# Seven products of a 2 x 2 block matmul, joined in two PSUM accumulators instead of four, and used for eight more columns of fc

## The chip, the core and the metric

The kernel runs on one core of a Trainium2 chip. Five engines work from queues of their own, each in the order in which the program issued its work: TensorE (PE, matmul), VectorE (DVE), ScalarE (ACT), GpSimd (POOL) and SyncE (SP, which here only issues DMAs). They wait for each other through semaphores. The metric is the device time of one execution in microseconds; lower is better. Before the change it is 803.75 us (median of three runs, 800.14 to 804.41).

## The reference

A cross-attention block on 4 batches, 512 query rows, 512 context rows, width 512, 16 heads of 32, inner width 2048, all in float32:

```python
x = layer_norm(hidden_states, ln1_w, ln1_b)
q, k, v = x @ q_w + q_b, enc @ k_w + k_b, enc @ v_w + v_b      # 16 heads of 32
attn = softmax(where(mask, q @ k.T / sqrt(32), min))
hidden = (attn @ v) @ cproj_w + cproj_b + hidden_states
y = layer_norm(hidden, ln2_w, ln2_b)
y = gelu(y @ fc_w + fc_b, approximate=True)                    # fc: 512 -> 2048
return hidden + y @ proj_w + proj_b                            # proj: 2048 -> 512
```

## The kernel before

**Attention.** The work is cut into 16 groups `w` (batch `w // 4`, four heads each) and each group into four query tiles `qt` of 128 rows: 64 *units* `u = 4 w + qt`. Each unit does, in this order of issue:

- `attend` (L331), in some units only: 16 matmuls that multiply exchanged probabilities of an earlier half group with v, and a VectorE multiply into `oT`;
- `scores` (L255): four matmuls into `sc`, four banks of PSUM of which there is one set (L259), so that the next unit's scores wait until VectorE has read all four. VectorE adds the mask and takes the row's extreme (L266), ScalarE takes the exponential (L270), four times each;
- `turn` (L274): VectorE transposes the probabilities; in odd units ScalarE makes `rr` (L292), and the *exchange* (L303, L314) sends 16 DMAs on SP that move blocks between partitions;
- *filler*: other TensorE work that hides the softmax. The lists `first[w]` and `later[w]` (L798 to L881) say by hand which work goes into which unit. A tuple gives one list for each `qt`; a plain list is spread over the group by the costs `CHAIN` and `TURN` (L718) and due times (L904 to L909).

Filler is made of the k, q and v products of later groups (`prep_k`, `prep_q`, `prep_v`), transposes, the output projection of a finished batch (`cproj`), and the MLP of batch 0 and half of batch 1 (`mlp`, L812 to L815). `some(n)` (L817) takes the next n matmul chains of the MLP; a pair of fc columns counts as two. `SPLIT` is 1: batch 0's whole MLP and the first half of batch 1's lie inside attention; the rest follows in `last_mlps` (L590).

**The MLP's fc.** The layer-normed rows, turned, are in `yT`; f counts 16 blocks of 128 columns of fc. There are two ways to compute it:

- `fc` (L532), for the first eight blocks of batch 1: one chain of four 128x512 matmuls a block, then gelu on ScalarE straight from PSUM (L537).
- `fc_seven` (L483), for *pairs* c of blocks: the 256 columns and 512 rows are seen as a 2 x 2 block product, for which seven products of half-size blocks do instead of eight. Each product is two 128x256 matmuls (L495). The weights' sums s1 to s4 are made by GpSimd in attention (`fc_sums`, L520, two pairs ahead) and by VectorE after it (`sum_wa`, L580); the sums t1, t2, t3, t4 of `yT` by `y_sums` (L472). t3 takes the place of a block of `yT`.

In `fc_seven` the seven products go into four PSUM tiles: q1; q2 and q6; q5 and q7; q3 and q4. ScalarE copies q1 to SBUF (L498), VectorE joins the rest in four sums (L501 to L509), and ScalarE applies gelu to two 128x512 halves (L513). In attention the tiles come from `ps_acc` (four banks, shared with every other chain), after it two come from `ps_acc` and two from `ps_last` (four banks). A PSUM tile of 512 floats is one bank.

`fc_by_pair` (L543) calls it in attention, `fc_pair` (L608) after it. `proj` (L551) is the second half of the MLP in attention (accp, L554); after attention `project` (L613) does it with seven products too.

**Queues that matter for the change.** GpSimd's queue also holds `v_bias` (L252), row sums on loaded rows (`add_row`, L357, which waits for the DMA of `load_hid`, L397), the layer norm's scale (`ln_rs`, L131) and some DMA issues. SP's queue holds all weight loads (`load_mlp`, L437, L444), `load_hid` (L402) and the exchanges (L328). ScalarE's table for the exponential and that for gelu alternate, with a table load each time.

**Batch 1 in attention.** In units 52 to 63 the filler is: five chains of proj of batch 0 (units 52 to 55), one more (56), then one fc chain in unit 57, two in 58, one in each of 59 to 62, one and a proj chain in 63. After the last unit come the other seven proj chains of batch 1, among them the last two attends.

Of the kernel before, what the change touches and what calls it, by code (L numbers as in the profile page):

```python
# [12 lines left out]
F32 = mybir.dt.float32  # L13
U8 = mybir.dt.uint8
AF = mybir.ActivationFunctionType
# [5 lines left out]
P = 128  # L21
# [4 lines left out]
ND = D // P  # L26
# [4 lines left out]
FQ = NF // NQ  # L31
# [3 lines left out]
SPLIT = 1  # L35
FIRST = 2
# [11 lines left out]
LN1W, LN1B, QB, KB, LN2W, LN2B, FCB = 0, 4, 8, 12, 16, 20, 24  # L48
# [4 lines left out]
def xattn_block(ctx: ExitStack, tc: tile.TileContext, x, encT, mask, q_w, k_w, v_w, c_w, fc_w, p_w, vecs, rows, out):  # L53
    nc = tc.nc
    scale = float(np.float32(1.0) / np.sqrt(HD).astype(np.float32))

    def pools(stack, **bufs):
        return [stack.enter_context(tc.tile_pool(name=n, bufs=k)) for n, k in bufs.items()]

    const, keep, hids, tiles, small = pools(ctx, const=1, keep=1, hids=6, tiles=4, small=4)  # L60
# [9 lines left out]
    vec = const.tile([P, NVEC], F32, tag="vec", name="vec")  # L70
# [3 lines left out]
    qb = const.tile([P, NG], F32, tag="qb", name="qb")  # L74
# [6 lines left out]
    gT = [gt[:, i * FQ * L : (i + 1) * FQ * L].rearrange("p (k l) -> p k l", k=FQ) for i in range(2)]  # L81
# [8 lines left out]
    ys = const.tile([P, 3, 2, L // 2], F32, tag="ys", name="ys")  # L90
# [6 lines left out]
    def mlp_w(n):  # L97
        n = n % MW + MW
        return pbt[:, n * D : (n + 1) * D]
# [16 lines left out]
    S = {}  # L116
    count = [0, 0, 0, 0, 0]
    Q = [nc.sync]

    def acc_tile(name):  # L120
        return ps_acc.tile([P, D], F32, tag="acc", name=name)
# [275 lines left out]
    def load_hid(b, ts_):  # L397

        for t in ts_:
            if ("hid", b, t) not in S:  # L400
                S["hid", b, t] = hids.tile([P, D], F32, tag="hid", name=f"hid_{b}_{t}")
            Q[0].dma_start(out=S["hid", b, t], in_=S["xa", b][ts(t, P), :])  # L402
        for t in ts_:
            add_row(S["hid", b, t], 1)

    def stat2(b, t):
        ln_stat((2, b), t, S["h", b, t])

    def norm2(b, t):
        h = S["h", b, t]  # L410
        y = tiles.tile([P, D], F32, tag="xn", name=f"xn2_{b}_{t}") if stays(b, t) else h
        S.setdefault(("yn", b), {})[t] = y
        ln_norm((2, b), t, y, h)
# [23 lines left out]
    def load_mlp():  # L437

        while count[0] < len(weights) and (count[0] < MW or weights[count[0] - MW][3] < count[1]):
            name, b, f, _ = weights[count[0]]  # L440
            w = mlp_w(count[0])
            if name == "fc":
                w = w.rearrange("p (d f) -> p d f", d=ND)
            Q[0].dma_start(out=w, in_=fc_w[:, f, :, :] if name == "fc" else p_w[ts(f, P), :])  # L444
            S[name + "w", b, f] = w
            count[0] += 1

    NP = NF // 2
    HL = L // 2

    def sub(o, x0, x1, engine=None):
        (engine or nc.vector).tensor_tensor(o, x0, x1, ALU.subtract)  # L452

    def add(engine, o, x0, x1):
        engine.tensor_tensor(o, x0, x1, ALU.add)  # L455
# [13 lines left out]
    def y_blocks(b):  # L469
        return [S["yT", b][:, 2 * k : 2 * k + 2, j * HL : (j + 1) * HL] for k in range(2) for j in range(2)]  # L470

    def y_sums(b):  # L472
        y11, y12, y21, y22 = y_blocks(b)
        e = nc.vector if b else nc.gpsimd
        sub(ys[:, 0], y12, y11)
        sub(ys[:, 1], y22, ys[:, 0])
        sub(y12, y22, y12, e)
        sub(ys[:, 2], y21, ys[:, 1], e)

    def acc_half(name):  # L480
        return acc_tile(name).rearrange("p (i l) -> p i l", i=2)

    def fc_seven(b, c, g, a, s, half):  # L483

        y11, t3, y21, y22 = y_blocks(b)
        t1, t2, t4 = (ys[:, i] for i in range(3))
        s1, s2, s3, s4 = s
        q1, q26 = (acc_half(f"{n}_{b}_{c}") for n in ("q1", "q26"))
        q57, q34 = (half(f"{n}_{b}_{c}") for n in ("q57", "q34"))
        p1 = small.tile([P, HL], F32, tag="p1", bufs=1, name=f"p1_{b}_{c}")  # L490
        g = g.rearrange("p i (j l) -> p (i j) l", j=2)

        def product(o, x, y):
            for k in range(2):
                nc.tensor.matmul(o, x[:, k], y[:, k], start=(k == 0), stop=(k == 1))  # L495

        product(q1[:, 0], a[0][:, 0:2], y11)
        nc.scalar.copy(p1, q1[:, 0])  # L498
        product(q26[:, 0], a[0][:, 2:4], y21)
        product(q26[:, 1], s2, t2)  # L500
        add(nc.vector, g[:, 0:4:3], q26, p1[:, None, :].broadcast_to([P, 2, HL]))  # L501
        product(q57[:, 1], s3, t3)
        product(q57[:, 0], s1, t1)
        u2 = g[:, 3:4]
        add(nc.vector, g[:, 1:3], q57, u2.broadcast_to([P, 2, HL]))
        add(nc.vector, g[:, 3], q57[:, 0], g[:, 2])
        product(q34[:, 0], s4, y22)
        product(q34[:, 1], a[1][:, 2:4], t4)
        add(nc.vector, g[:, 1:3], q34, g[:, 1:3])  # L509
        for i in range(2):  # L510
            f = 2 * c + i
            h = g[:, 2 * i : 2 * i + 2]
            nc.scalar.activation(h, h, AF.Gelu_apprx_tanh, bias=vec[:, FCB + f : FCB + f + 1], scale=1.0)  # L513

    fc_pairs = [(b, c) for b in range(SPLIT) for c in range(NP)]

    def raw_pair(b, c):
        return [S["fcw", b, 2 * c + i] for i in range(2)]

    def fc_sums():  # L520

        while count[3] < len(fc_pairs) and count[3] < count[4] + 2:
            b, c = fc_pairs[count[3]]
            if ("fcw", b, 2 * c + 1) not in S:
                return
            x, y = raw_pair(b, c)
            s = wsum[:, count[3] % 2]
            a_sums(x[:, :2], x[:, 2:], y[:, :2], y[:, 2:], s[:, 0], s[:, 1], y[:, :2], s[:, 2], nc.gpsimd)
            S["ws", b, c] = s[:, 0], s[:, 1], y[:, :2], s[:, 2]
            count[3] += 1  # L530

    def fc(b, f):  # L532
        q, k = divmod(f, FQ)
        acc = acc_tile(f"accf_{b}_{f}")
        for d in range(ND):
            nc.tensor.matmul(acc, S["fcw", b, f][:, d, :], S["yT", b][:, d, :], start=(d == 0), stop=(d == ND - 1))  # L536
        nc.scalar.activation(  # L537
            gT[q % 2][:, k, :], acc, AF.Gelu_apprx_tanh, bias=vec[:, FCB + f : FCB + f + 1], scale=1.0
        )
        count[1] += 1  # L540
        load_mlp()

    def fc_by_pair(b, c):  # L543
        q, k = divmod(2 * c, FQ)
        fc_seven(b, c, gT[q % 2][:, k : k + 2, :], raw_pair(b, c), S["ws", b, c], acc_half)
        count[1] += 2
        count[4] += 1
        load_mlp()
        fc_sums()
# [40 lines left out]
    def last_mlps():  # L590
# [76 lines left out]
                add(nc.vector, hid(1, 0, t), q4[t][:, t], hid(1, 0, t))  # L667
                nc.sync.dma_start(out=out[b, ts(2 + t, P), :HL], in_=hid(1, 0, t))

        y_sums(SPLIT)  # L670

        half = FIRST * FQ // 2
        for b, pairs, new in (
            (SPLIT, range(half, NP), ()), (SPLIT + 1, range(NP), range(half)), (SPLIT + 2, range(NP), ())
# [43 lines left out]
    CHAIN, TURN = 3.4, 0.5  # L718

    def do(fn):  # L720
        return [(0.0, fn)]

    def A(w):
        if w >= NW:
            return []
        return [
            (CHAIN, lambda: prep_k(w)),
            (CHAIN, lambda: prep_q(w)),
            (CHAIN, lambda: prep_v(w)),
        ]  # L730

    def C(b):
        return [(CHAIN, lambda t=t: cproj(b, t)) for t in range(NT)]
# [5 lines left out]
        return [(TURN, lambda d=d: ln2_turn(b, d)) for d in range(ND)]  # L739

    def FC(b, q):
        if b < SPLIT:
            return [(2 * CHAIN * 7 / 8, lambda c=c: fc_by_pair(b, c)) for c in range(q * FQ // 2, (q + 1) * FQ // 2)]
        return [(CHAIN, lambda f=f: fc(b, f)) for f in range(q * FQ, (q + 1) * FQ)]

    def PJ(b, q):
        return [(CHAIN, lambda t=t: proj(b, q, t)) for t in range(NT)]
# [50 lines left out]
    first = [[] for _ in range(NW)]  # L798
# [18 lines left out]
    def some(n):  # L817
        taken = []
        while n > 0:
            n -= 1 if mlp[0][0] == CHAIN else 2  # L820
            taken.append(mlp.pop(0))
        assert n == 0
        return taken

    def hid_(b, *ts_):
        return do(lambda: load_hid(b, ts_))
# [10 lines left out]
    def rs(b):  # L837
        return do(lambda: ln_rs((2, b)))

    def stat(b, *ts_):  # L840
        return do(lambda: [stat2(b, t) for t in ts_])

    def norm(b, *ts_):
        return do(lambda: [norm2(b, t) for t in ts_])
# [3 lines left out]
    k, q, v = A(7)  # L848
    c, t2 = C(0), turns2(0)
    first[4] = x1 + [k, q, v] + x4  # L850
    later[4] = c[:1] + x2[:1] + c[1:2] + x2[1:2] + c[2:3] + x2[2:] + c[3:]
    k, q, v = A(8)
# [3 lines left out]
    k, q, v = A(9)  # L856
    x1, x2, x3, x4 = inputs(3)
    first[6] = [k, q] + some(4) + [v] + x1
    k, q, v = A(10)
    first[7] = [k, q] + x2[:1] + some(2) + x2[1:2] + some(2) + [v]  # L860

    k, q, v = A(11)
    first[8] = h_(1, 0, 1) + x2[2:] + [k, q] + x3[:2] + some(2) + x3[2:3] + [v] + x3[3:] + h_(1, 2, 3) + x4
    later[8] = cb(1) + C(1)
    k, q, v = A(12)
    first[9] = [q] + some(2) + [k] + some(2) + [v]
    k, q, v = A(13)
    first[10] = [k, q] + some(4) + [v]
    k, q, v = A(14)
    t2 = turns2(1)  # L870
# [5 lines left out]
    k, q, v = A(15)  # L876
    c = C(2)
    first[12] = [k, q], cb(2) + [v], c[:2], c[2:]
    first[13] = some(1), some(1) + stat(2, 0, 1), some(1) + stat(2, 2, 3) + rs(2), some(2)
    first[14] = some(1) + norm(2, 0, 1), some(1) + norm(2, 2, 3), some(2), some(1)  # L880
    first[15] = hid_(1, 2, 3) + some(1), some(1), some(1), some(2)  # L881

    for w in range(NW):
        if w and w % NG == 0:
# [42 lines left out]
    c = C(B - 1)  # L927
# [49 lines left out]
```

## Time and profile before

| what | value |
|---|---|
| runs | 800.14, 804.41, 803.75 us |
| profiled execution: its own time / span from first to last instruction | 801.93 / 800.2 us |
| mean granted TensorE clock | 0.998 |
| attention | 0 to about 535 us of the span |
| after it: batch 3's output projection, then fc and proj of what is left | 535 to 800 us |
| 195 to 430 us: PE / DVE / ACT / POOL busy, of 235.0 | 234.66 / 188.59 / 130.86 / 38.62 us |
| 430 to 500 us, of 70.0 | 69.10 / 63.46 / 49.01 / 5.45 us |
| 549 to 800 us, of 251.0 | 247.24 / 143.40 / 37.01 / 29.68 us |
| matmuls in `fc_seven` (L495), records, mean of one | 784 records (28 pairs x 14 matmuls x 2), 379 or 380 ns |
| matmuls in `fc` (L536) | 64 records, 604 ns |
| ScalarE copy of q1 (L498) | 28, 355 ns |
| VectorE joins of a pair after attention (L455) | 684, 692, 692 and 425 ns |
| GpSimd sums of weights (L455, L452), 128x256 | 32, 735 to 750 ns |

How to read it: a float32 matmul leaves two records ("pieces") in the trace, each with its weight load, and the pieces overlap in the array, so that a piece of 379 ns is followed by the next after some 216 ns; a busy TensorE is therefore not a measure of its speed, but a gap between pieces is one of its waiting. "Idle before, releaser" gives how long an engine stood still ahead of an instruction and what ended that.

### The profile page before, as it was taken

The page shows a single profiled execution, that of the slowest core. Times are in us where ns is not written, and L with a number is a line of the kernel's source. Part 1 is how long each engine was busy: PE and PEld are TensorE (multiplying, and loading weights), DVE is VectorE, ACT ScalarE, POOL GpSimd, SP SyncE. Part 2 cuts the span into 40 slices and gives each one's busy share as a digit, 9 for nine tenths or more (in the row PEclk, how much of TensorE's full clock was granted, in tenths as well). Part 3 has the DMA queues.
Part 4 walks back from the last instruction along what each step waited for, and adds up shares of the span by engine and source line. Part 5 has one row for each costly group of instructions (what it writes and reads, how often), then busy time and mean ns, then how long its engine had stood idle before and what let it go on. Part 6 is the DMA issues. An engine that isn't in the chain of part 4 may idle for free.

```text
span 800.2 us, 12085 instructions
## 1 busy us (share of the span) xinstructions
PE 785.3 (98%) x4178; PEld 499.4 (62%) x4178; DVE 573.8 (72%) x1179; ACT 339.5 (42%) x745; POOL 123.9 (15%) x146
## 2 busy tenths in 40 slices
PE   9999999989999999999999999999999999999998
PEld 6545455456655645556553433446888888888887
DVE  3789998888888857779878988546738983368511
ACT  2567765547763636456554479500201220022100
POOL 1210030055121141001220100020040020200011
PEclk9999999999999999999999999999999999999999
DMA  8889999847897777787777799882325330033001
GB/s 325 289 230 241 235 237 244 231 115 182 209 240 196 211 210 192 179 198 199 181 173 213 205 261 246 202 254 93 117 84 172 118 106 14 27 86 86 1 14 40
DMA packets 60957, 137.15 MB, mean 171 GB/s; under 512 B 12464, under 2 KB 15664, under 8 KB 60768
## 3 DMA queue, kind: packets, MB, share of 16 engines
q1 hardware_dynamic: 59472, 132.43, 61.3%
q0 software_dynamic: 896, 2.82, 1.1%
q10 hardware_dynamic: 528, 1.14, 0.7%
q8 instruction: 33, 0.54, 0.3%
q14 instruction: 28, 0.23, 0.1%
HBM read 58.22 MB, written 6.82 MB: 81 GB/s over the span
## 4 chain that ended last, share of the span: by engine, by line
PE 87%; DVE 6%; SPq 3%; ACT 1%; issue 1%; DMA 1%; POOL 0%; DVEq 0%; POOLq 0%; ACTq 0%
PE q L495 20%; PE accp L554 8%; PE sc L262 7%; PE accc L386 7%; PE av L345 7%; PE accv L240 6%; PE acck L218 6%; PE accq L228 5%; PE accf L536 3%; DVE ptt L266 3%; SPq L328 2%; PE q4p L622 2%; PE q3p L622 2%; PE q5p L622 2%; PE q6p L622 2%; PE q7p L622 2%
## 5 line engine op out<-in xcount | busy, mean ns | idle before, releaser
L270 ACT ACTIVATE ptt<-ptt,mn 128x512 f32<-128x512 f32 x256 | 181.7, 711 | 135.1 <-DVE mn L266 134.8
L266 DVE CUSTOM_DVE_ANT_0 ptt<-sc,mb 128x512 f32<-128x512 f32 x256 | 161.0, 685 | 32.7 <-PE sc L262 32.4
L285 DVE STREAM_TRANSPOSE tb<-ptt 128x1024 f32<-128x1024 f32 x96 | 119.2, 1242 | 14.4 <-ACT ptt L270 12.9
L554 PE MATMUL accp<-pbt,gt 128*128 128x512 f32 x192 | 86.7, 600 | 0.0
L495 PE MATMUL q<-yT,gt 128*128 128x256 f32 x320 | 78.9, 379 | 0.0
L262 PE MATMUL sc<-pbt 32*128 32x512 f32 x512 | 73.0, 640 | 4.7 <-DVE mn L266 2.5
L513 ACT ACTIVATE ga<-ga,vec 128x512 f32<-128x512 f32 x40 | 26.7, 714 | 93.2 <-DVE ga L455 93.2
L495 PEld LDWEIGHTS q<-yT,gt 128*128 128x128 f32 x320 | 60.8, 190 | 8.7 <-issue 0.5
L554 PEld LDWEIGHTS accp<-pbt,gt 128*128 128x128 f32 x192 | 35.2, 190 | 49.0 <-issue 46.4
L240 PEld LDWEIGHTS accv<-ptt,xe 128*128 128x128 f32 x512 | 58.7, 192 | 9.5 <-issue 6.7
L495 PE MATMUL q<-ys,gt 128*128 128x256 f32 x240 | 61.8, 380 | 0.5 <-DVE ys L452 0.5
L240 PE MATMUL accv<-ptt,xe 128*128 128x128 f32 x512 | 60.8, 277 | 0.0
L218 PE MATMUL acck<-xe,ptt 128*128 128x512 f32 x128 | 59.1, 605 | 0.0
L228 PE MATMUL accq<-xe,ptt 128*128 128x512 f32 x128 | 58.4, 599 | 0.0
L386 PE MATMUL accc<-wc,oT 128*128 128x512 f32 x128 | 56.6, 596 | 0.0
L495 PEld LDWEIGHTS q<-ys,gt 128*128 128x128 f32 x240 | 45.4, 190 | 7.4 <-DVE ys L452 0.9
L345 PE MATMUL av<-pT,v 128*32 128x256 f32 x768 | 48.1, 392 | 1.8 <-DMA gt<-tb 0.7
L498 ACT COPY p<-q 128x256 f32<-128x256 f32 x28 | 9.9, 355 | 92.5 <-PE q L495 92.5
L270 ACT ACTIVATION_READ_ACCUMULATOR ptt<-ptt,mn 128x1 f32 x256 | 47.8, 187 | 0.0
L252 POOL TENSOR_TENSOR v<-v,row 128x512 f32<-128x512 f32 x16 | 20.4, 1275 | 172.9 <-ACT v L245 172.8
L228 PEld LDWEIGHTS accq<-xe,ptt 128*128 128x128 f32 x128 | 23.6, 190 | 32.4 <-issue 30.4
L262 PEld LDWEIGHTS sc<-pbt 32*128 32x128 f32 x512 | 20.0, 182 | 37.9 <-issue 21.4
(137 smaller groups left out, 1071.4 us busy)
## 6 DMA issues: line engine op xcount, KB each, us to landing
pT<-tb SPq DMA_DIRECT2D x384, 136.0 KB, 2.4
pbt<-p_w_dram SPq DMA_DIRECT2D x40, 256.0 KB, 3.1
gt<-fc_w_dram SPq DMA_DIRECT2D x40, 256.0 KB, 2.6
gt<-tb SPq DMA_DIRECT2D x64, 136.0 KB, 3.4
xe<-tb SPq DMA_DIRECT2D x56, 136.0 KB, 3.1
pbt<-fc_w_dram SPq DMA_DIRECT2D x24, 256.0 KB, 3.9
ptt<-k_w_dram SPq DMA_DIRECT2D x16, 256.0 KB, 3.8
xe<-encT_dram SPq DMA_DIRECT2D x16, 256.0 KB, 4.6
```

Source lines behind the costliest of these rows:

```text
L218: nc.tensor.matmul(acc, S["wk", w][:, d, :], eT[:, d, :], start=(d == 0), stop=(d == ND - 1))
L228: nc.tensor.matmul(acc, S["wq", w][:, d, :], xT[:, d, :], start=(d == 0), stop=(d == ND - 1))
L240: nc.tensor.matmul(acc[:, ts(t, P)], eT[:, d, ts(t, P)], S["wv", w][:, d, :], start=(d == 0), stop=(d == ND - 1),)
L262: nc.tensor.matmul(sc[:, h, :], qT[r, ts(qt, P)], kT[r, :], start=True, stop=True)
L266: nc.vector.tensor_tensor_reduce(out=s, in0=sc[:, h, :], in1=S["mb", w // NG], scale=1.0, scalar=FMAX, op0=ALU.add, op1=ALU.min, accum_out=mn,
L270: nc.scalar.activation(s, s, AF.Exp, bias=mn, scale=-1.0, accum_out=sums[:, qt, h : h + 1])
L285: nc.vector.transpose(*two_heads[k])
L345: nc.tensor.matmul(av[ts(h, HD), : 2 * P].rearrange(shape, **kw), v[:, t, ts(h, HD)], p[t][h], start=(t == 0), stop=(t == NT - 1),)
L386: nc.tensor.matmul(acc, S["oT", b][:, g, ts(t, P)], wc[:, g, :], start=(g == 0), stop=(g == NG - 1))
L495: nc.tensor.matmul(o, x[:, k], y[:, k], start=(k == 0), stop=(k == 1))
L554: nc.tensor.matmul(acc, gT[q % 2][:, k, ts(t, P)], S["pw", b, q * FQ + k], start=(k == 0), stop=(k == FQ - 1))
L622: nc.tensor.matmul(o[:, t], a[:, c, ts(t, P)], w[:, c], start=(c == pairs[0]), stop=(c == pairs[-1]))
```

## The change

`fc_seven` joins the products in two PSUM tiles, qa and qb. TensorE adds two products onto others in the same accumulator: q3 onto q5 and q4 onto q7 in qb, q2 onto q1 in qa. Between them ScalarE copies qb (q5 and q7, 128x512) and the lower half of qa (q1, 128x256) to SBUF. GpSimd makes two of the sums (128x256), VectorE two (128x256, 128x512). Gelu is three instructions, one of them from PSUM. The order of the products is q5, q7, q1, q6, q3, q4, q2.

The first half of fc of batch 1 is done by pairs too (four pairs instead of eight chains), and `fc` is gone. For that GpSimd makes the weight sums of these four pairs (`fc_pairs`) and `y_sums(1)` in unit 52; before, VectorE made `y_sums(1)` after attention. The filler of units 52 to 63 is dealt out anew: unit 57 and 58 have a pair each, 60 and 62 too, 59 and 61 have none, 63 has two proj chains.

```diff
     def y_sums(b):
         y11, y12, y21, y22 = y_blocks(b)
-        e = nc.vector if b else nc.gpsimd
-        sub(ys[:, 0], y12, y11)
-        sub(ys[:, 1], y22, ys[:, 0])
-        sub(y12, y22, y12, e)
-        sub(ys[:, 2], y21, ys[:, 1], e)
+        e, o = ((nc.vector, nc.gpsimd), (nc.gpsimd,) * 2)[b] if b <= SPLIT else (nc.vector,) * 2
+        sub(ys[:, 0], y12, y11, e)
+        sub(ys[:, 1], y22, ys[:, 0], e)
+        sub(y12, y22, y12, o)
+        sub(ys[:, 2], y21, ys[:, 1], o)
...
-        q1, q26 = (acc_half(f"{n}_{b}_{c}") for n in ("q1", "q26"))
-        q57, q34 = (half(f"{n}_{b}_{c}") for n in ("q57", "q34"))
-        p1 = small.tile([P, HL], F32, tag="p1", bufs=1, name=f"p1_{b}_{c}")
+        qa, qb = acc_half(f"qa_{b}_{c}"), half(f"qb_{b}_{c}")
         g = g.rearrange("p i (j l) -> p (i j) l", j=2)
+        u2 = g[:, 0]
 
-        def product(o, x, y):
+        def product(o, x, y, clear=False):
             for k in range(2):
-                nc.tensor.matmul(o, x[:, k], y[:, k], start=(k == 0), stop=(k == 1))
+                nc.tensor.matmul(o, x[:, k], y[:, k], start=clear and k == 0, stop=k == 1, skip_group_check=not clear)
 
-        product(q1[:, 0], a[0][:, 0:2], y11)
-        nc.scalar.copy(p1, q1[:, 0])
-        product(q26[:, 0], a[0][:, 2:4], y21)
-        product(q26[:, 1], s2, t2)
-        add(nc.vector, g[:, 0:4:3], q26, p1[:, None, :].broadcast_to([P, 2, HL]))
-        product(q57[:, 1], s3, t3)
-        product(q57[:, 0], s1, t1)
-        u2 = g[:, 3:4]
-        add(nc.vector, g[:, 1:3], q57, u2.broadcast_to([P, 2, HL]))
-        add(nc.vector, g[:, 3], q57[:, 0], g[:, 2])
-        product(q34[:, 0], s4, y22)
-        product(q34[:, 1], a[1][:, 2:4], t4)
-        add(nc.vector, g[:, 1:3], q34, g[:, 1:3])
-        for i in range(2):
+        product(qb[:, 0], s1, t1, True)
+        product(qb[:, 1], s3, t3)
+        nc.scalar.copy(g[:, 2:], qb)
+        product(qa[:, 0], a[0][:, 0:2], y11, True)
+        nc.scalar.copy(u2, qa[:, 0])
+        product(qa[:, 1], s2, t2)
+        add(nc.gpsimd, g[:, 3], g[:, 2], g[:, 3])
+        add(nc.vector, u2, qa[:, 1], u2)
+        add(nc.gpsimd, g[:, 3], g[:, 3], u2)
+        product(qb[:, 0], s4, y22)
+        product(qb[:, 1], a[1][:, 2:4], t4)
+        add(nc.vector, g[:, 1:3], qb, u2[:, None, :].broadcast_to([P, 2, HL]))
+        product(qa[:, 0], a[0][:, 2:4], y21)
+        for i, o, x in ((0, g[:, 1], g[:, 1]), (0, g[:, 0], qa[:, 0]), (1, g[:, 2:], g[:, 2:])):
             f = 2 * c + i
-            h = g[:, 2 * i : 2 * i + 2]
-            nc.scalar.activation(h, h, AF.Gelu_apprx_tanh, bias=vec[:, FCB + f : FCB + f + 1], scale=1.0)
+            nc.scalar.activation(o, x, AF.Gelu_apprx_tanh, bias=vec[:, FCB + f : FCB + f + 1], scale=1.0)
 
-    fc_pairs = [(b, c) for b in range(SPLIT) for c in range(NP)]
+    fc_pairs = [(b, c) for b in range(SPLIT + 1) for c in range(NP if b < SPLIT else FIRST * FQ // 2)]
...
-    def fc(b, f):
...
-    def fc_by_pair(b, c):
+    def fc(b, c):
         q, k = divmod(2 * c, FQ)
         fc_seven(b, c, gT[q % 2][:, k : k + 2, :], raw_pair(b, c), S["ws", b, c], acc_half)
...
-        y_sums(SPLIT)
-
         half = FIRST * FQ // 2
...
-    first[13] = some(1), some(1) + stat(2, 0, 1), some(1) + stat(2, 2, 3) + rs(2), some(2)
-    first[14] = some(1) + norm(2, 0, 1), some(1) + norm(2, 2, 3), some(2), some(1)
-    first[15] = hid_(1, 2, 3) + some(1), some(1), some(1), some(2)
+    first[13] = do(lambda: y_sums(1)) + some(1), some(1) + stat(2, 0, 1), some(1) + stat(2, 2, 3) + rs(2), some(2)
+    first[14] = some(1) + norm(2, 0, 1), norm(2, 2, 3) + some(2), some(2), []
+    first[15] = hid_(1, 2, 3) + some(2), [], some(2), some(2)
```

## The prediction

> **What bounds the kernel now.** I read the page first: busy shares, then the chain that ended last.
>
> ```profile
> PE 785.3 (98%) x4178; PEld 499.4 (62%) x4178; DVE 573.8 (72%) x1179; ACT 339.5 (42%) x745; POOL 123.9 (15%) x146
> PE 87%; DVE 6%; SPq 3%; ACT 1%; issue 1%; DMA 1%; POOL 0%; DVEq 0%; POOLq 0%; ACTq 0%
> ```
>
> TensorE sets the time: in the chain the first 224 pieces of fc from 700.25 take 48.35 us, 0.216 us a piece (a matmul is two pieces), no gap. So TensorE work removed is time won, and a wait put into TensorE's order is time lost unless TensorE would have waited there anyway. Next the timeline at a pair inside attention:
>
> ```profile
> 202.28 1.14 PE L262 MATMUL sc<-pbt 32*128 32x512 f32 x8
> 203.35 1.99 PE L495 MATMUL q<-yT,pbt 128*128 128x256 f32 x8
> 203.49 0.69 DVE L266 CUSTOM_DVE_ANT_0 ptt<-sc,mb 128x512 f32<-128x512 f32 x1 [1.02 <-PE sc L262]
> 204.23 0.72 ACT L270 ACTIVATE ptt<-ptt,mn 128x512 f32<-128x512 f32 x1 [1.15 <-DVE mn L266]
> ...
> 207.74 0.36 ACT L498 COPY p<-q 128x256 f32<-128x256 f32 x1
> ```
>
> The scores go out, the pair follows at once on TensorE (203.35), but ScalarE must first do four exponentials that wait for VectorE, and reaches the pair's copy 4.4 us after the pair began. In the old order that harms nobody: nothing later in the pair needs the copied bank.
>
> **The change, part by part.** *Matmuls.* Four pairs take the place of eight fc chains of batch 1. A chain after scores takes 3.63 us on the chain of waits (478.29), a pair 6.24 (203.42): 8 x 3.63 - 4 x 6.24 = **4 us less** on TensorE. The other pairs keep their 28 pieces.
>
> *The new wait.* In the changed program's order the first matmul of s2·t2 (upper half of qa) waits for the ScalarE copy of q1 (lower half of qa): they share a PSUM bank. That copy stands behind the new 128x512 copy of qb, and TensorE's order holds everything behind it. So in all 32 pairs: q1 ends, ScalarE copies, TensorE goes on. [...]
>
> Price with ScalarE free, from rows where TensorE and ScalarE hand over:
>
> ```profile
> 20.57 1.02 PE L228 MATMUL accq<-xe,ptt 128*128 128x512 f32 x2
> 21.62 0.69 ACT L231 ACTIVATE pbt<-accq,qb 128x512 f32<-128x512 f32 x1 [2.66 <-PE accq L228]
> 22.36 1.14 PE L262 MATMUL sc<-pbt 32*128 32x512 f32 x8 [0.78 <-ACT pbt L231]
> ```
>
> 0.03 us to ScalarE, 0.05 back. The last piece lasts 0.38 (379 ns mean), the copy 0.35 (L498), the restart 0.10 (8 pieces from 203.35: 1.99 against 7 x 0.216 + 0.38 = 1.89). Less the normal step: 0.38 + 0.03 + 0.35 + 0.05 + 0.10 - 0.216 = **0.70 us a pair**. In the 20 pairs after attention ScalarE is free in time: VectorE's join (0.69) of the pair before starts one product (0.86) ahead of that pair's end, the gelu that waits for q2 follows 0.2 after the end, and 0.36 + 0.71 more finish all three 1.3 us into the new pair; the copy of qb has its data only at 1.95 (8 pieces and the last one's length). 20 x 0.70 = **+14**. VectorE loses 2.49 - 1.11 = 1.4 us a pair there (684 + 2 x 692 + 425 against about 420 + 690 ns), which buys nothing: TensorE did not wait for it. Bounds: 0.5 to 1.0 a pair.
>
> *The eight pairs of batch 0.* With A from pair start to ScalarE's old copy, the qb copy adds 0.49 (577 ns of L245's 128x512 copy, less 0.09 overlap), then 0.35 + 0.05 + 0.10; q1 would have ended its turn at 2.69. Stall = A - 1.70. A is 3.7, 4.4, 4.5, 4.4, 4.5, 4.7 in six pairs (177.97, 203.35, 212.53, 268.89, 305.35, 373.08): 2.0, 2.7, 2.8, 2.7, 2.8, 3.0. At 351.04 ScalarE is idle: 0.7. At 185.28 the old A of 6.6 came from gelus that waited for three late sums; now pair 0 ends at 186.1, its gelus at 187.5, the table load (1.28) at 188.8, the unit's exponentials and rr at 192.4, while pair 1 starts at 187.2: A = 5.2, stall 3.5. Sum **+20**. From 195 to 430 TensorE is busy 234.7 of 235.0 us, so there is no idle time for the stalls to fill. If VectorE's and ScalarE's catching up took half of it: +10.
>
> *Batch 1 in attention (units 57 to 63).* GpSimd now runs y_sums(1) and both pairs' weight sums ahead of the layer-norm scale of batch 2. Weights issued 453.66 land after 3.9 (median): 457.5; eight sums of 0.74 end 463.4; then a store 0.54, 0.2, 1.03: 465.3, where norm on VectorE started at 463.34. VectorE and the exponentials of unit 57 come 2 us later, ScalarE is free at 470.95, and pair 0 (start 462.55, A = 8.4) stalls 6.7 and ends 475.5. Pair 1 starts after one set of scores at 476.5; gelus (1.4), table load (1.28) and four exponentials (3.0) free ScalarE at 481.2: A = 4.7, stall 3.0. Units 59 and 61 have an attend but no filler, so after unit 59's scores TensorE waits until VectorE has read the four score banks: 0.1 + 4 x 0.61, 2.6. Pair 2 starts at 492.3, but VectorE transposes unit 59 until 494.2; reads and exponentials end 497.9: A = 5.6, stall 3.9. Then GpSimd's order:
>
> ```profile
> 483.75 10.05 SPq L328 DMA_DIRECT2D xe<-tb  x16
> ...
> 494.55 0.86 SPq L402 DMA_DIRECT2D hid<-xa  x2
> ```
> ```profile
> 497.76 1.27 POOL L357 TENSOR_TENSOR hid<-hid,row 128x512 f32<-128x512 f32 x1 [33.32 <-DMA hid<-xa]
> 501.96 1.27 POOL L357 TENSOR_TENSOR hid<-hid,row 128x512 f32<-128x512 f32 x1 [2.93 <-DMA hid<-xa]
> ```
>
> GpSimd waits idle for a load that SP issues only after an exchange of 10 us; pair 2's two GpSimd sums now stand behind it, VectorE's join must wait for the first of them, and the scores of unit 61 behind that. With the exchange from 494.2 to 504.3 the second load (issued 504.9, 4.9 the median of these two) lands at 509.8; its row sum 1.27, the first of pair 2's sums 0.73, the join 0.69, oT 0.4, four reads 2.5: the scores of unit 62 start at 515.3 where those of unit 61 ended 505.4, a wait of 9.9. The transposes of unit 61 then hold the reads of unit 62: A = 6.8 in pair 3, stall 5.1. Stalls 6.7 + 3.0 + 2.6 + 3.9 + 9.9 + 5.1 = 31.2, less 0.9 that stood at 467.15 before, less the 4 saved: **+26**. With the load out of the way, 9.9 becomes 2.6 and 5.1 the 3.9 of pair 2: +18; with the later landing (6.8, the longer of the two) +28.
>
> *The clock.* One idle of 3.05 us cost speed:
>
> ```profile
> 172.68 0.66 PE L159 MATMUL tp<-ident,xn 128*128 128x128 f32 x4 [3.05 <-ACT pbt L231]
> 173.35 3.61 PE L345 MATMUL av<-pT,v 128*32 128x256 f32 x32
> ```
>
> That attend takes 3.61 where others take 1.93; the clock from 165 to 180 is 0.89. I take two such losses of 1.7 (behind the 6.7 and the 9.9): **+3**; bounds 0 to 8 losses, 14. [...]
>
> *Gone.* The 0.7 us wait of an attend on ScalarE's copy (192.28) and 0.7 at 549.61, where fc waited for y_sums: **-1**.
>
> Sum: 801.9 (the profiled execution, span 800.2 and 1.7 around it) + 14 + 20 + 26 + 3 - 1 = **863 us**. The median of the runs is 1.8 higher than that execution; I leave that inside the range.
>
> **Rivals.** (a) *Attention absorbs it*: a stalled TensorE lets VectorE and ScalarE catch up, A shrinks from pair to pair, GpSimd is not blocked. For: VectorE is 80% busy there and is often released by TensorE. Against: A is made of the unit's own exponentials (0.75 + 4 x 0.72 and the rr copy), which start only with its scores. Price: 14, half of 20, 18 less 10, none of the clock: 801.9 + 32 - 1 = 833. (b) *Faster*: the wait is free and only the matmuls count: 801.9 - 4 - 1 = 797. It needs ScalarE to have copied q1 within one piece (0.216 us) after q1's last, or the bank wait to be absent; the copy alone takes 0.35. (c) *GpSimd becomes the bound*: its sums (0.73 each, in series: copy, sum, VectorE, sum, gelu) hold ScalarE's gelus in the last 20 pairs too, and so the next pair's copy. It decides when the second sum ends over 1.2 us after the pair (1.95 less the last gelu's 0.71); by the rows it ends 1.1 before the pair does (VectorE's sum 2.0 before, 0.1 and 0.73). Price: each 1 us beyond that point is paid 20 times, 883.
>
> **How the numbers follow.** Forecast 863: 0.72. (a) 833: 0.16. (c) 883: 0.08. (b) 797: 0.03; no change: 0.01. The range: below, 863 less 8 (load not blocked), 10 (half of batch 0), 3 (clock), 4 (0.2 a pair) gives 838; above, 2 (late landing), 10 (clock), 4 give 880. A measurement of this kernel can tell 0.5%, 4 us, from no change. Faster 0.03, same 0.01, slower 0.96.
>
> **What would show it.** After: TensorE idle before s2·t2 in every pair, ended by the ScalarE copy; 0.6 to 0.7 us in each of the last 20, 2 to 3 in attention, so TensorE's busy share below 94%; gelus of pair 2 of batch 1 ended by GpSimd, and GpSimd by the hid load; about 60 us lost in all, two fifths of it in units 57 to 63 (461 to 504 of the old time). Wrong if the stretch after attention is as long as before (then the bank wait costs nothing), or if units 57 to 63 are under 12 us longer.

## The result and the profile after

| | before | after |
|---|---|---|
| runs on the same chip, us | 804.08 median (800.14 to 805.32, 4 runs) | **874.39** median (869.73 to 875.58, 4 runs) |
| ratio, 95% interval | 1 | **1.0873** [1.0818, 1.0927] |
| span of the profiled execution, us | 800.2 | 873.8 |
| mean granted TensorE clock | 0.998 | 0.975 |

The forecast was 863, its range 838 to 880: the time lies inside, 11 us above the forecast. The page of the kernel after, in the order in which the prediction read that of before: busy shares, TensorE's granted clock over the span (40 slices), the chain that ended last.

```profile
PE 804.7 (92%) x4226; PEld 516.3 (59%) x4226; DVE 539.9 (62%) x1127; ACT 360.1 (41%) x809; POOL 186.2 (21%) x230
...
PEclk9999999988999999999999998899999999999999
...
PE 72%; DVE 10%; SPq 7%; ACT 6%; DMA 2%; issue 2%; POOL 1%; DVEq 0%; POOLq 0%
```

TensorE, 98% busy before, stands still for 8% of the span, and its part of the chain fell from 87% to 72%. Its busy time rose by 19 us although it has less to compute: the slices with an 8 in the clock's row are where it worked at a lower clock. The view of TensorE's waits says for whom it stood still (total us, times, longest):

```profile
PE qa L494 <- ACT gt L500: 30.6, 11, 5.3
PE sc L262 <- DVE mn L266: 14.3, 3, 10.0
PE qa L494 <- ACT ga L500: 9.2, 20, 0.5
```

L494 is the matmul in `fc_seven`, L500 ScalarE's copy of q1. The wait stands ahead of q6, which is s2\*t2. TensorE adds three products (q3, q4 and q2, not two) onto others in PSUM; q6 is none of them, but shares q1's bank. The first line is the pairs inside attention (`gt`), the third the 20 pairs after it (`ga`). The second, scores that wait for VectorE, was 2.5 us in two waits before.

The stretches of the span, cut at the first scores of units 22, 57 and 63 and at the first fc matmul after attention; TensorE's starts in the traces give the cuts:

| us | units 22 to 57 (batch 0's MLP) | 57 to 63 (batch 1's pairs) | 63 to fc | last 20 pairs and projects |
|---|---|---|---|---|
| before | 284.6 | 38.2 | 49.9 | 250.5 |
| after | 313.6 | 70.2 | 46.5 | 266.0 |
| difference | **+29.0** | **+32.0** | -3.4 | **+15.5** |

Now one pair of the last stretch, TensorE's timeline (start, us, what, idle before):

```profile
690.32 1.03 PE L494 MATMUL qb<-yT,gt 128*128 128x256 f32 x4
691.19 1.03 PE L494 MATMUL qa<-yT,gt 128*128 128x256 f32 x4
692.67 1.13 PE L494 MATMUL qa<-ys,gt 128*128 128x256 f32 x4 [0.46 <-ACT ga L500]
```

q1 goes out at 691.19, and s2\*t2 would have followed after four steps of 0.216, at 692.05; it starts at 692.67, 0.62 late, and with 0.10 of restart a pair takes 6.77 us where it took 6.04. That is the new wait, 20 times. One pair of this stretch pays another one: its first product, which is now q5, needs a sum of weights, and waits for VectorE to make it:

```profile
662.27 1.13 PE L494 MATMUL qb<-ys,gt 128*128 128x256 f32 x4 [1.06 <-DVE gt L455]
```

In the old order q1 came first, which needs no sum. (Below, "stall" is such a gap between two pieces' starts less the normal step of 0.216; the trace's own idle figure is smaller, since a piece still runs while the next could have started.)

In units 57 to 63 the chain through GpSimd stands in four timelines of the kernel after. SyncE first:

```profile
524.13 11.10 SPq L328 DMA_DIRECT2D xe<-tb  x16
535.34 1.01 SPq L402 DMA_DIRECT2D hid<-xa  x2
```

GpSimd:

```profile
538.39 2.48 POOL L357 TENSOR_TENSOR hid<-hid,row 128x512 f32<-128x512 f32 x2 [20.57 <-DMA hid<-xa]
540.83 1.52 POOL L455 TENSOR_TENSOR gt<-gt 128x256 f32<-128x256 f32 x2
```

VectorE:

```profile
541.59 0.69 DVE L455 TENSOR_TENSOR gt<-qb,gt 128x512 f32<-128x512 f32 x1 [11.45 <-POOL gt L455]
542.19 0.41 DVE L350 TENSOR_TENSOR oT<-av,pT 128x256 f32<-128x256 f32 x1
```

and TensorE:

```profile
533.99 1.14 PE L262 MATMUL sc<-pbt 32*128 32x512 f32 x8
545.10 2.09 PE L262 MATMUL sc<-pbt 32*128 32x512 f32 x8 [9.97 <-DVE mn L266]
```

SyncE issues an exchange for 11.10 us and only then the load; GpSimd, idle for 20.57 us, waits for it with pair 2's sums behind it; VectorE's join waits for them, the scores' readers stand behind the join, and TensorE waits 9.97 us. The scores that follow take 2.09 us instead of 1.14: they run at half clock (granted: 0.50 from 537.4 to 551.1).

### The profile page after: what moved, and what is told of

The parts are those of the page before. It is cut to its first block, busy times and chain, and to the rows that moved or that the text cites. A ratio compares the mean times of both kernels' runs of the same rounds, so it can differ in the third digit from the quotient of the medians.

```text
span 873.8 us, 12245 instructions
## 1 busy us (share of the span) xinstructions
PE 804.7 (92%) x4226; PEld 516.3 (59%) x4226; DVE 539.9 (62%) x1127; ACT 360.1 (41%) x809; POOL 186.2 (21%) x230
## 3 DMA queue, kind: packets, MB, share of 16 engines
q10 hardware_dynamic: 528, 1.14, 0.6%
## 4 chain that ended last, share of the span: by engine, by line
PE 72%; DVE 10%; SPq 7%; ACT 6%; DMA 2%; issue 2%; POOL 1%; DVEq 0%; POOLq 0%
PE qb L494 11%; PE qa L494 9%; PE accp L541 7%; SPq L328 7%; PE accc L386 6%; PE av L345 6%; PE sc L262 5%; PE accv L240 5%; DVE ptt L266 5%; PE acck L218 4%; PE accq L228 3%; ACT ptt L270 2%; DVE tb L285 2%; PE q5p L609 2%; PE q3p L609 2%
## 5 line engine op out<-in xcount | busy, mean ns | idle before, releaser
L455 POOL TENSOR_TENSOR ga<-ga 128x256 f32<-128x256 f32 x40 | 29.0, 726 | 137.5 <-ACT ga L498 94.8
L511 ACT ACTIVATE ga<-ga,vec 128x256 f32<-128x256 f32 (+1 forms) x40 | 24.4, 609 | 73.8 <-DVE ga L455 73.8
L498 ACT COPY ga<-qb 128x512 f32<-128x512 f32 x20 | 11.7, 587 | 103.5 <-PE qb L494 60.6
L494 PE MATMUL qa<-ys,wsum 128*128 128x256 f32 x48 | 17.7, 504 | 31.1 <-ACT gt L500 30.6
L386 PEld LDWEIGHTS accc<-wc,oT 128*128 128x128 f32 x128 | 23.7, 190 | 31.5 <-issue 29.1
L494 PE MATMUL qb<-ys,gt 128*128 128x256 f32 x160 | 41.2, 380 | 1.1 <-DVE gt L455 1.1
```

Of the source, the lines that this page charges most:

```text
L386: nc.tensor.matmul(acc, S["oT", b][:, g, ts(t, P)], wc[:, g, :], start=(g == 0), stop=(g == NG - 1))
L494: nc.tensor.matmul(o, x[:, k], y[:, k], start=clear and k == 0, stop=k == 1, skip_group_check=not clear)
```

## The experiments

Theory A, the prediction's: three causes, which add: the bank of qa shared by a ScalarE read and TensorE's next write (all 32 pairs); units 57 to 63, where the new pairs wait for ScalarE, two units have no filler and GpSimd stands behind a load; and the clock, lost where TensorE is idle. Rival B: the time comes from elsewhere, from GpSimd's and ScalarE's added work or the new order of products, or it goes from one wait into the next. The stretches of all kernels, cut as above, with the time that the half clock cost (half of TensorE's busy time while the granted clock was 0.5):

| us | median | 22 to 57 | 57 to 63 | 63 to fc | last | half clock |
|---|---|---|---|---|---|---|
| before | 804.1 | 284.6 | 38.2 | 49.9 | 250.5 | 1.7 |
| after | 874.4 | 313.6 | 70.2 | 46.5 | 266.0 | 17.6 |
| e_own_bank | 837.5 | 296.2 | 65.3 | 46.5 | 250.8 | 7.5 |
| e_acc_alone | 845.5 | 309.4 | 38.2 | 51.5 | 267.0 | 5.0 |
| e_pairs_alone | 813.3 | 286.8 | 51.0 | 46.5 | 249.9 | 5.0 |
| e_hid_later | 863.2 | 308.4 | 62.7 | 46.5 | 265.9 | 12.4 |
| e_own_hid | 828.7 | 297.3 | 57.6 | 46.5 | 250.8 | 11.2 |
| e_q1_thrice | 863.8 | 306.3 | 65.9 | 46.5 | 266.1 | 3.5 |
| e_q1_first | 861.3 | 304.0 | 71.1 | 46.5 | 263.0 | 13.0 |
| e_q1_mid | 854.0 | 309.1 | 70.2 | 46.5 | 251.6 | 19.5 |
| e_dealt | 809.9 | 285.5 | 44.0 | 51.0 | 249.8 | 3.3 |
| e_dealt_tail | 807.1 | 285.8 | 43.7 | 47.9 | 249.9 | 3.4 |

**1. q1 in a bank of its own** (e_own_bank).

```diff
-        qa, qb = acc_half(f"qa_{b}_{c}"), half(f"qb_{b}_{c}")
+        qa, qb, qc = acc_half(f"qa_{b}_{c}"), half(f"qb_{b}_{c}"), acc_half(f"qc_{b}_{c}")
...
-        product(qa[:, 0], a[0][:, 0:2], y11, True)
-        nc.scalar.copy(u2, qa[:, 0])
-        product(qa[:, 1], s2, t2)
+        product(qc[:, 0], a[0][:, 0:2], y11, True)
+        nc.scalar.copy(u2, qc[:, 0])
+        product(qa[:, 1], s2, t2, True)
...
-        product(qa[:, 0], a[0][:, 2:4], y21)
+        product(qc[:, 0], a[0][:, 2:4], y21)
```

(the gelu that reads q2 reads it from qc.)

> The changed kernel (874.4 us) with q1 and q2 in a PSUM tile of their own, so that s2 t2 no longer shares a bank with the copy of q1; order, engines and sums stay. Theory A (the bank wait in TensorE's order is the loss): no wait ahead of s2 t2 any more; the 20 pairs after attention go back to 6.04 us each (15 us less); in attention TensorE now waits only ahead of s4 y22 for the copy of qb, some 1.1 us less in each of 12 pairs (13 less), and with stalls under 2 us most half-clock stretches of batch 0 go (6 to 10 less): 836 us, 828 to 848. Theory B (GpSimd's sums in series and the new dealing of the units are the loss, the bank is not): 868 to 876.

Measured: 837.46 us, ratio 1.0408 [1.0386, 1.0430], inside theory A's range. All of the last stretch's loss is gone (a pair takes 6.04 us again). In attention a stall stays, now one product later, at s4\*y22 (q3) into qb, which ScalarE's other copy still reads (waits of TensorE in this kernel):

```profile
PE qb L494 <- ACT gt L498: 17.3, 11, 4.6
PE sc L262 <- DVE mn L266: 15.0, 3, 10.7
```

There is no line of such a wait with `ga`. So a bank of its own for q1 and q2 takes away 37 us of the 70 (15 in the last stretch, 17 in batch 0, 5 in units 57 to 63; 10 of them are time at half clock), and theory A holds. It is not all that sharing costs: at qb TensorE still waits 17.3 us. q1 and q6 lie in one tile as well as in one bank, so the runs don't tell a wait for the tile from one for the bank, and none shows what would happen without the wait.

**2. Each half of the change alone.** e_acc_alone is the kernel before with the new `fc_seven` and nothing else of the change:

```diff
-        q1, q26 = (acc_half(f"{n}_{b}_{c}") for n in ("q1", "q26"))
-        q57, q34 = (half(f"{n}_{b}_{c}") for n in ("q57", "q34"))
...
+        qa, qb = acc_half(f"qa_{b}_{c}"), half(f"qb_{b}_{c}")
...
```

e_pairs_alone is the kernel after with the `fc_seven` of before, the same lines the other way round, so that the pairs of batch 1, their sums and the new deal of the units are left.

> The kernel before (804 us) with the changed fc_seven alone: batch 1's first half stays with eight plain chains, the units stay dealt as before, y_sums of batch 1 stays on VectorE after attention. Theory A: 0.74 us in each of 20 pairs after attention and 29 us in the eight pairs of batch 0 (20 of stalls, 10 of half clock): 848 us, 842 to 854. Theory B (the new units and GpSimd's queue make the loss): under 820.

> The changed kernel with the old fc_seven (four PSUM tiles): the four pairs of batch 1, their weight sums and y_sums on GpSimd, and the new dealing of units stay. Theory A: no wait inside a pair, GpSimd makes no sum of products and so blocks nobody; left are two waits of 2.6 us in units 59 and 61, 2 us for the late layer-norm scale, less 4 of matmuls saved: 808 us, 800 to 815. Theory B: the new dealing costs most of it: over 825.

Measured: 845.53 us, 1.0511 [1.0488, 1.0533], and 813.26 us, 1.0108 [1.0083, 1.0133], both inside theory A's ranges. The accumulators alone leave units 57 to 63 as they were (38.2) and cost nearly as much as in the kernel after in batch 0 (309.4) and as much in the last stretch (267.0). The eight stalls of batch 0 are those of the kernel after to 0.02 us; but only three of them were followed by half clock here, five there, which is most of the 4.2 us between the two. The pairs alone cost 12.8 us in units 57 to 63 and give 3.4 back behind them. The two add up to 49 us (40.7 + 8.4, each against the 804.86 us of before on that chip), the whole change to 70: some 21 us arise only together, 19 of them in units 57 to 63, where the new pairs have the new waits (70.2 against 51.0).

**3. The load behind the pair** (e_hid_later).

```diff
-    first[15] = hid_(1, 2, 3) + some(2), [], some(2), some(2)
+    first[15] = some(2) + hid_(1, 2, 3), [], some(2), some(2)
```

> The changed kernel with load_hid of batch 1 issued behind pair 2 instead of ahead of it in unit 60, so that pair 2's GpSimd sums no longer stand behind the row sums that wait for that load. Theory A (the 10.0 us wait of TensorE ahead of unit 62's scores comes from that queue): that wait falls to about 2.6, the 13.7 us at half clock shrink: 862 us, 856 to 868. Theory B (the wait comes from VectorE's and ScalarE's own backlog): no change, 871 to 877.

Measured: 863.24 us, 1.0734 [1.0710, 1.0759], 11 less than after: theory A's range. TensorE's timeline of this kernel at the place of the 9.97:

```profile
529.52 1.14 PE L262 MATMUL sc<-pbt 32*128 32x512 f32 x8
533.32 2.09 PE L262 MATMUL sc<-pbt 32*128 32x512 f32 x8 [2.66 <-DVE mn L266]
```

Moving one load behind pair 2's GpSimd sums shortens the wait to the 2.66 that a unit without filler costs anyway. Not all of the 11 us are the load's. In the profiled executions units 57 to 63 fell by 7.5 us; batch 0, which the edit does not touch, fell by 5.2: its stalls are the same, but three were followed by half clock instead of five, and an attend's wait of 1.3 us for a DMA is missing.

**4. Both repairs** (e_own_hid: the edits of 1 and 3).

> Both repairs in one: q1 and q2 in a PSUM tile of their own (as in the experiment of that name, 837.5 us) and the load of the residual rows of batch 1 behind the pair of unit 60 (as in the experiment of that name, 11 us less than the kernel after). Theory (the bank wait and GpSimd's blocking are separate costs that add): 826 to 831 us. Rival (the blocking costs only because the bank wait has put the units late): 835 to 838.

Measured: 828.70 us, 1.0307 [1.0284, 1.0330], inside the theory's range. The load gives 8.8 us here, 7.7 of them in units 57 to 63: two separate costs.

**5. The clock** (e_q1_thrice). More TensorE work is put where TensorE stands still; it computes q1 two times more and changes nothing in the result.

```diff
-        product(qa[:, 0], a[0][:, 0:2], y11, True)
+        for _ in range(3 if half is acc_half else 1):
+            product(qa[:, 0], a[0][:, 0:2], y11, True)
```

> The kernel after, with the product q1 issued three times in each of the 12 pairs in attention (the same result, written over; four more matmuls, 8 pieces of 0.216 us, 1.72 us of TensorE work a pair that computes nothing new). Theory (the idle time before s2*t2 is what drops the granted clock): the copy of q1 ends when it did, since ScalarE comes to it from its exponentials, so the added work lies inside the idle time, the idle becomes 0.2 to 1.2 us, the stretches at half clock in batch 0 (units 22 to 57, five of 3.4 us in the kernel after) go, and with the one pair that has no idle time to fill (+1) the time is 860 to 868 us: TensorE does 20 us more work in less time. Rival (the clock stretches come from something else, such as the load itself): the half clock stays, the time is 874 to 882.

Measured: 863.79 us, 1.0759 [1.0728, 1.0790]: with 20 us **more** work for TensorE, 10.6 us less than after. In batch 0 no stretch at half clock is left (five in after). The same place in the two kernels, pair 4: in after its s2\*t2 stood idle for 2.52 us and then ran at half clock (2.05 us instead of 1.10),

```profile
288.40 2.05 PE L494 MATMUL qa<-ys,wsum 128*128 128x256 f32 x4 [2.52 <-ACT gt L500]
```

and in the experiment:

```profile
278.37 1.13 PE L494 MATMUL qb<-ys,wsum 128*128 128x256 f32 x4
279.34 1.03 PE L494 MATMUL qb<-yT,pbt 128*128 128x256 f32 x4
280.20 2.75 PE L494 MATMUL qa<-yT,pbt 128*128 128x256 f32 x12
283.75 1.10 PE L494 MATMUL qa<-ys,wsum 128*128 128x256 f32 x4 [0.80 <-ACT gt L501]
284.69 1.03 PE L494 MATMUL qb<-yT,wsum 128*128 128x256 f32 x4
```

s2\*t2 comes 5.4 us after the pair's start in both, as ScalarE lets it, but only 0.80 of them are idle here, and the clock stays at 1. Here the idle time, not the load, cost the clock; the rival falls.

**6. q1 first** (e_q1_first), then with VectorE's queue put in order (e_q1_mid).

```diff
+        product(qa[:, 0], a[0][:, 0:2], y11, True)
+        nc.scalar.copy(u2, qa[:, 0])
         product(qb[:, 0], s1, t1, True)
         product(qb[:, 1], s3, t3)
         nc.scalar.copy(g[:, 2:], qb)
-        product(qa[:, 0], a[0][:, 0:2], y11, True)
-        nc.scalar.copy(u2, qa[:, 0])
         product(qa[:, 1], s2, t2)
```

> The kernel after with the products in the order q1, q5, q7, q6, q3, q4, q2, and the ScalarE copy of q1 ahead of that of qb. Theory (TensorE waits only for the copy of q1, and what counts is when that copy ends against the end of the third product): in the last 20 pairs ScalarE copies q1 while TensorE makes q5 and q7 (1.73 us), so their 0.74 us each go, -15; in attention the copy ends 0.49 earlier (no copy of qb ahead of it) and TensorE comes to s2*t2 at the same time as before, so each of the 12 stalls is 0.5 shorter, -6, and fewer of them are long enough to cost clock, 0 to -6. Then the first piece of s4*y22 must wait for the copy of qb, which ends 0.6 after q1's: s2*t2 (0.43) covers most of it, +0.2 in attention. Sum 848 to 854 us. Rival (any ScalarE copy between products that share a bank costs the same, wherever it stands): 868 or more.

Measured: 861.34 us, 1.0698 [1.0670, 1.0727]: between the two, 7 above the theory's end. Batch 0 gave what was expected (the seven stalls that remain are 0.5 shorter each, 14.9 us together with the eighth gone instead of 19.0, and two were followed by half clock instead of five). Units 57 to 63 gave nothing (71.1 for 70.2; pair 0's stall grew from 5.5 to 6.2; why stays open), and the last stretch gave 3 of 15. Its timelines, TensorE and then VectorE:

```profile
661.05 1.03 PE L494 MATMUL qb<-ys,gt 128*128 128x256 f32 x4
662.63 1.99 PE L494 MATMUL qa<-yT,gt 128*128 128x256 f32 x8 [0.55 <-DVE ga L455]
```

```profile
660.58 0.53 DVE L455 TENSOR_TENSOR gt<-gt 128x256 f32<-128x256 f32 x1 [3.02 <-DMA gt<-fc_w_dram]
661.04 1.21 DVE L452 TENSOR_TENSOR gt<-gt 128x256 f32<-128x256 f32 x3
662.16 0.42 DVE L455 TENSOR_TENSOR ga<-qa,ga 128x256 f32<-128x256 f32 x1
```

The wait has a new owner, in 14 of the 20 pairs: q2 must now wait until VectorE has read qa (662.16), and that join stands behind the weight sums of the next pair, which wait for their load. In after the join ended 0.5 us before q2, covered by the very stall that the new order took away. So the second edit: the four sums behind the join.

```diff
         add(nc.vector, u2, qa[:, 1], u2)
+        sums()
...
-            sums()
             fc_seven(b, c, ga[:, c], [wa[c % 2][:, i] for i in range(2)],
-                     [ws[c % 2][:, i] for i in range(4)], half_tile)
+                     [ws[c % 2][:, i] for i in range(4)], half_tile, sums)
```

> The order of the products as in the experiment with q1 first (861.3 us), and in the last 20 pairs VectorE makes the next pair's weight sums after its join of q1 and q6 instead of before it. There, in 13 of the 20 pairs, TensorE stood 0.72 us (and 0.10 of restart) before y21, the last product into qa, waiting for that join, which stood on VectorE behind four sums of weights that wait for their load. Theory (that queue is the whole of it): 13 x 0.82 = 10.7 us go, less what VectorE's last join and the gelus come later, up to 0.15 a pair: 850 to 854 us. Rival (q1 first moves the wait from one reader of the bank to the next, whatever VectorE's order): 858 to 864.

Measured: 853.97 us, 1.0629 [1.0604, 1.0655], at the end of the theory's range. The last stretch falls from 263.0 to 251.6, nearly before's 250.5. Units 22 to 57 were 5.1 us longer than in e_q1_first, with the same stalls to 0.02 us: three stalls of 2.2 us were followed by half clock here and not there (see the last section).

**7. Pairs in attention without empty units** (e_dealt, e_dealt_tail; four-tile `fc_seven`; the lines that differ from e_pairs_alone).

```diff
-    mlp += FC(SPLIT, 0) + FC(SPLIT, 1) + PJ(SPLIT, 0) + PJ(SPLIT, 1)
+    mlp += FC(SPLIT, 0) + PJ(SPLIT, 0) + FC(SPLIT, 1) + PJ(SPLIT, 1)
...
-    first[14] = some(1) + norm(2, 0, 1), norm(2, 2, 3) + some(2), some(2), []
-    first[15] = hid_(1, 2, 3) + some(2), [], some(2), some(2)
+    first[14] = some(1), some(2), some(2) + norm(2, 0, 1) + hid_(1, 2, 3), some(1) + norm(2, 2, 3)
+    first[15] = some(1), some(1), some(1), some(2)
```

(the weights are loaded in the same new order.)

> The four-tile fc_seven of before, the four pairs of batch 1 in attention as in the kernel after, but no unit without filler: proj chains follow each half of fc (fc half 0, proj half 0, fc half 1, proj half 1), so that units 57 and 58 have a pair each, 59 to 62 a proj chain each, and 63 a pair; the load of the residual rows stands in unit 58. Theory (what the four-tile form loses in units 57 to 63, 12.8 us by its experiment, comes from the empty units and from GpSimd behind the load): 798 to 806 us, where the 4 us that the pairs save on TensorE show up if all of it goes. Rival (pairs in these units cost because VectorE and ScalarE have too much to do there): 809 to 815.

Measured: 809.89 us, 1.0074 [1.0057, 1.0091]: the rival's range. Units 57 to 63 are 7 us shorter than in e_pairs_alone, but 5.8 longer than before. Some 1.4 of that is matmul work that lay elsewhere before (two pairs and four chains for seven chains). The rest is waiting: from 461 to 500 us VectorE is busy for 35.8 of 39.0 us and TensorE for 34.3 (before: 33.4 and 38.1); an attend waits 1.4 us for ScalarE's copy, and three units' scores wait 0.7 to 1.7 us for VectorE, the longest here:

```profile
493.67 1.14 PE L262 MATMUL sc<-pbt 32*128 32x512 f32 x8 [1.66 <-DVE mn L266]
```

VectorE makes the pairs' joins there; a chain of the old `fc` needed none. That the joins are what holds the scores is read from the queue; no run took them away. And ScalarE's queue held a surprise, shown by its timeline and then TensorE's:

```profile
517.20 5.85 ACTq L328 DMA_DIRECT2D xe<-tb  x7
523.42 0.37 ACT L498 COPY p<-q 128x256 f32<-128x256 f32 x1 [5.66 <-DMA xe<-tb]
```

```profile
523.85 3.62 PE L345 MATMUL av<-pT,v 128*32 128x256 f32 x32 [4.00 <-ACT p L498]
```

The last exchange is issued in part by ScalarE, and the pair's copy stands behind it; an attend waited 4.0 us for the copy. The last run puts that pair ahead of the exchange:

> The redealt four-tile kernel (809.9 us), with the pair that came after the last exchange put ahead of it. In that kernel ScalarE reached this pair's copy of q1 5.7 us late, because ScalarE's queue issues 8 of the last exchange's DMAs ahead of the copy; an attend then waited 4.0 us and ran at half clock (3.62 us instead of 1.93). Theory (that queue is the cost): 5.7 us go, 803 to 806 us. Rival (the last exchange is now late instead, and the last attend waits for it): 808 to 812.

Measured: 807.13 us, 1.0049 [1.0032, 1.0066], between the two. The 4.0 and the half clock behind it went, but 1.9 us came back as a wait of proj for its weights, which SyncE now loads later:

```profile
528.17 11.40 PE L543 MATMUL accp<-pbt,gt 128*128 128x512 f32 x26 [1.95 <-DMA pbt<-p_w_dram]
```

No version here beats the kernel before.

## Why the prediction was right, and where it was short

Measured against its own terms, from the gaps and the stretches:

| step | predicted | measured |
|---|---|---|
| last 20 pairs, 0.70 each | +14 | +15.5 (20 x 0.73 of bank wait and 1.2 at one q5, less the 0.6 for y_sums that went) |
| batch 0, stall A - 1.70, eight pairs | +20: 2.0, 3.5, 2.7, 2.8, 2.7, 2.8, 0.7, 3.0 | +19.8: 1.9, 3.5, 2.7, 2.0, 2.7, 2.8, 0.7, 2.7 and 0.1 restart each |
| batch 1, stalls and waits | 31.2: 6.7, 3.0, 2.6, 3.9, 9.9, 5.1 | 26.8: 5.5, 2.9, 2.7, 3.4, 10.0, 2.4 |
| less the old wait and the saved matmuls | -0.9, -4 | -0.9, -0.8 inside and -3.4 behind |
| clock | **+3** | **+16** |

- *The bank wait* was right in mechanism and size: experiment 1 takes it away, experiment 2 has it alone. The rows of before in which the two engines hand over priced it at 0.70; a pair shows 0.73 (6.77 against 6.04). The 1.2 us at one pair's q5 belong to the new order of products, and the sum had no term for them.
- *A is not shortened by the stalls* (rival a, 833): six of batch 0's eight stalls came within 0.1 us of what was worked out from the old times of ScalarE's copy; the other two were 0.8 and 0.3 shorter.
- *Batch 1*: GpSimd behind the load came at 9.97 for 9.9, and experiment 3 shows the cause. The stalls of pairs 0 and 3 were shorter than worked out (5.5 for 6.7, 2.4 for 5.1). Pair 3 began at half clock, so its own products used up part of the time until ScalarE's copy; why pair 0's was shorter was not tested. Neither of the two signs that would have spoken against the mechanism came: the stretch after attention grew by 15.5, units 57 to 63 by 32.0.
- *The clock is the step that failed*: "I take two such losses of 1.7 (behind the 6.7 and the 9.9)". Half of TensorE's busy time at half clock is 17.6 us, less before's 1.7: 16. The stretches say the same: batch 0 is 29.0 longer and its stalls are 19.8, which leaves 9.2; units 57 to 63 are 32.0 longer, and 26.8 - 0.9 - 0.8 leaves 6.9. I had reserved the loss for the long stalls; stalls of 2.7 to 3.5 us cost it in five of the eight pairs of batch 0. Even the bound, 14, was short.
- *Luck*: how many of equal stalls cost the clock differs. The same eight stalls of batch 0 were followed by half clock five times in after and three times each in e_acc_alone and e_hid_later, 1.7 us a time, and of the four runs of after the shortest, 869.7 us, had a mean granted clock of 0.980, the others 0.975 or 0.976. And two misses had opposite signs: the clock took 13 us more than forecast, batch 1's stalls and matmuls 4 to 5 less, so that a part of the clock's miss does not show in the total.
- *Rival c* (GpSimd holds the last 20 pairs) did not come in the kernel after; e_q1_first shows that its neighbour lay close: VectorE's queue held 14 of the same pairs as soon as the order of products changed.
- *Rival b* (797) falls with the bank wait. That the pairs' four saved microseconds could be kept in attention was tried in experiment 7: waits took them back, by the timeline mostly those for VectorE.

## What to carry to other kernels

Here, joining products in one accumulator, or only putting them into one bank, made the engine that reads a part of the bank a link in TensorE's order (0.73 us a pair with ScalarE free, 0.7 to 5.5 in attention): price it by where that engine's copy stands in its queue, not by how long the copy takes. When a stall is removed, ask which read of a shared bank is next; here it was late by less and hidden behind the first (the copy of qb, 17.3 us in e_own_bank). Stalls of 2.2 us were followed by half clock in e_q1_mid (three of three; in e_q1_first none of three), those of 1.9 and 2.0 in after were not, and such a stretch cost some 1.7 us, so count short stalls too. And where a comparison of two profiles shows a gain in a stretch that the edit did not touch, look at the clock there first.

## What the runs showed of the hardware

**In these traces the granted clock changed on a grid of 3.413 us, and a window of that grid that was some 60% idle was enough to halve it.** In the twelve profiled executions the granted clock changes only on this grid, the same all through one execution (in after the stretches at half clock last 3.41, 6.83 and 13.65 us). The grid was laid over the trace, and TensorE's busy time in each window was set against the clock of the next:

| TensorE busy in a window at full clock, us | next at full clock | next at half clock |
|---|---|---|
| under 1.4 | 0 | 48 |
| 1.4 to 1.6 | 11 | 3 |
| 1.6 to 1.8 | 19 | 1 |
| 1.8 and more | 2676 | 0 |

(the windows from 20 us on; busy is the union of the matmuls in the trace.) So the line lies between 1.4 and 1.8 of 3.413 us (41% to 53% busy) in these traces, and the window did not have to be idle throughout (in after eight of the nine under 1.4 were busy for 0.90 to 1.30 us). In windows at half clock it was much the same amount of work: with busy/2 under 1.4 all 17 were followed by half clock, over 1.6 all 46 by full. So in these traces some 2 us of idle time (3.41 - 1.4) cost the clock where one window held them, and not where a window's edge cut them; a stall, as measured here, is about 0.16 longer than its idle time. That fits the equal stalls of 2.2 us, which did so in e_q1_mid (three of three) and not in e_q1_first (none of three). One such stall, in e_q1_first and then in e_q1_mid:

```profile
282.32 1.10 PE L494 MATMUL qa<-ys,wsum 128*128 128x256 f32 x4 [2.03 <-ACT gt L497]
```
```profile
283.88 1.66 PE L494 MATMUL qa<-ys,wsum 128*128 128x256 f32 x4 [2.04 <-ACT gt L497]
285.33 1.91 PE L494 MATMUL qb<-yT,wsum 128*128 128x256 f32 x4
```

In e_q1_first an edge of the grid at 281.19 cuts the idle time; in e_q1_mid the window from 280.87 to 284.28 holds all of it, TensorE is busy for 1.38 us of it, and the half clock begins at its end. The explanation by the edge is drawn from these traces; no run moved a stall against the grid on purpose.
